# A four-block transformer in one launch: background pieces are no longer issued between the score passes of the second block's attention

## The chip, the cores and the metric

The kernel runs on one core of a Trainium2 chip. The core has a matrix engine (TensorE, "PE" in the profile, with its weight loads as "PEld"), a vector engine (VectorE, DVE), an activation engine (ScalarE, ACT), a general engine (GpSimd, POOL) and a queue that issues transfers (SyncE, SP). Each engine works off its own instructions in the order in which the program was written; semaphores order them among each other. The metric is the time of one execution on the device in microseconds (us), as the median of several runs.

## The reference, cut to what matters

Four blocks are computed one after the other on 2048 tokens of 128 numbers. Each is attention of some kind and a feed-forward part, each with a layer norm in front and its input added:

```python
    x = L0_attn_x
    x = x + _L0_attn_ref(_layernorm(x, axis=-1), ...)   # 16 heads of 8
    x = x + _L0_ffn_ref(_layernorm(x, axis=-1), ...)    # gelu, 128 -> 512 -> 128
    x = x + _L1_attn_ref(_layernorm(x, axis=-1), ...)   # 16 heads of 64
    x = x + _L1_ffn_ref(_layernorm(x, axis=-1), ...)    # gated silu, 128 -> 384 -> 128
    x = x + _L2_attn_ref(_layernorm(x, axis=-1), ...)   # each token with its two neighbours
    x = x + _L2_ffn_ref(_layernorm(x, axis=-1), ...)    # router, the best of 8 experts
    x = x + _L3_attn_ref(_layernorm(x, axis=-1), ...)   # memory with a recurrence over chunks of 64
    x = x + _L3_ffn_ref(_layernorm(x, axis=-1), ...)    # router, the best 2 of 8 experts, and a shared one
    return x
```

The attentions of the first two blocks are over all 2048 tokens:

```python
        scores = q @ k.T * scale
        attn = softmax(scores)
        out = attn @ v
```

The memory of the last block is a recurrence. Its state is carried through 32 chunks of 64 tokens: in each, the gradient of a small network's loss is taken at the state, limited in its norm, and the state moves on by it. So a chunk can't begin before the one ahead of it has ended.

## The kernel before

**Stages.** The first block's attention (`l0_attn`) comes first, with its feed-forward part and the keys and values of the second block as work in the background. Then comes the second block's attention (`l1_attn`). Its queries are cut into five blocks `QB` of 384 (392 with some edge tokens), 512, 512, 384 and 256 tokens, and its 16 heads into 8 pairs. A unit is one query block with one pair of heads; there are 40 units in the order of `SEG`. A unit has 16 steps, one for each 128 keys.

**A step.** The scores are built transposed (keys on partitions, queries along the row), for both heads `e` of the pair, in four passes `ops`: the keys' high part by the queries' high part `qhh`, by their low part `qlt`, the keys' low part by `qhh`, and the subtraction of the row maximum (`onr` by `mbt`). ACT takes the exponential into `P`. POOL (in some steps DVE) adds up the rows' sums (`do_sum`, tiles `acg` and `acd`). The products with the values (`do_pv`) of two steps are made together (`pvn=2`): in a step called `last` here (every second one, and the first) the two earlier steps' products follow. `max_upto` computes the row maxima of a unit ahead: a product of queries and keys `km` and a `TENSOR_REDUCE` into `mx` on DVE.

**Banks.** The eight PSUM banks belong to one pool `mx`. Everything that multiplies takes one (`mi`, `take`) and gives it back (`rel`).

**Background.** What comes after the attention of a finished query block is cut into pieces by generators: `stage_a` and `stage_a2` (the gated feed-forward part and the next attention's inputs), `stage_b`, `stage_b2` (neighbour attention, experts), `stage_c`, `chunk`, `stage_d` (the recurrence: coefficients, 32 chunks, output), `stage_g` (the last router). A piece ends at a `yield`. What it yields tells what the next piece needs: an int is a number of banks, "T" says that the next piece holds a product but takes no bank, "same" that it follows on DVE, a fraction that it must wait so long. The last feed-forward part (`s_lane`, `stage_e0`) runs only in the tail, when attention has ended.

**The order.** All instructions are written by one Python program, in one order; the program keeps an estimated clock `clk` for each engine. `fill(lim, only)` issues background pieces: it goes through `helpers` (pieces that belong to units: query products, maxima, the ends of units) and `parts` (the generators above, in the order of `order`), takes the first whose `may` says that it is ready by the clocks, and goes on until the clock of PE has advanced by `lim` or nothing is ready. With `only="t"`, pieces that need a bank or hold a product (`banks`, `pe`) are passed over, so that PE's order is not changed. `need` issues what must be done by now, ready or not. At a unit's end (`u_end`) the rows' sums go through DRAM to be inverted and spread (`smd`, `rcd`, `rb`), and after every second unit `stage_wo` multiplies by the output weights; its last part adds to the residual `xs` and lets the background have the block.

**Where pieces are issued in `l1_attn`.** After each of the first three passes (`ti`) with "t"; after the exponentials, in a `last` step with a full `fill()` behind the maxima and then with "t", in the others with "t" alone; after each `do_pv` with "t"; and behind the products with a full `fill()` and "t" again.

The functions as the profile numbers them:

Of the kernel before, what the change touches and what calls it, by code (L numbers as in the profile page):

```python
# [28 lines left out]
CH = 64  # L29
NCH = S // CH  # L30
ATANH = (1.0000000039388743, 0.3333315796754013, 0.20012426861749952, 0.13980709417165652, 0.14087328632693624)
T = dict(ti=(0, 1, 2), tf=1, lead0=22, more0=4, mgap=0.4, pvq=2, lim0=0.5, fq=(3,), pl=-0.5, pr=1.0, tlow=2, tback=3, late=0.3, pvp="mx", mxp="mx", ex=(256, 768, 1280, 1792, 2047), low=1, lows='ge', keep=1, leave=5, pvn=2, sp=0, rdy=40., eu=2, qg=(22, 16, 10), em=2, el=6, sem=0.2, same=1.2, tsame=3.0, order="hdmBbAaEcCeg", ps=dict(mx=8), dma=2.3, slack=0.1, lim=0.6, backlog=2.5, lead=(10, 8, 6), pp=9, dve=(6, 7, 14, 15), qp=(1, 1), lanes=2, xl=5,
         QB=[(0, 384, 392), (384, 512, 512), (896, 512, 512), (1408, 384, 384), (1792, 256, 256)])


# [35 lines left out]
def body(ctx: ExitStack, tc: tile.TileContext, x, pa, pb, pc, pi, pd, pr, pr0, pe, pw, out):  # L71
# [16 lines left out]
    leave = [0]  # L88
    mode = [None]
    L1COST = {"T": (0.0, 1 / 2400), "A": (0.12, 1 / 1200), "D": (0.1, 1 / 960), "P": (0.15, 1 / 530)}  # L90
    COST = {"T": (0.0, 1 / 2400), "A": (0.09, 1 / 1200), "D": (0.04, 1 / 960), "P": (0.15, 1 / 460)}

# [3 lines left out]
    def note(eng, op, a, k):  # L96
# [7 lines left out]
        if eng == "S":  # L104
            clk["S"] = max(clk["S"], clk["T"]) + 0.55
            end = max(t, clk["S"]) + T["dma"]
        else:
            big = max(ins + outs, key=lambda v: math.prod(v.shape[1:])) if eng != "T" else outs[0]
            cols = math.prod(big.shape[1:])
            if eng == "T":  # L110
                cols *= 2 if op == "transpose" else 4 if ins[-1].dtype == F32 else 1
# [25 lines left out]
    class Eng:  # L137
# [3 lines left out]
        def __getattr__(self, name):  # L141
            f = getattr(self.e, name)

            def g(*a, **k):
# [7 lines left out]
    te, ve, se, ge, sy = (Eng(e, n) for e, n in ((nc.tensor, "T"), (nc.vector, "D"), (nc.scalar, "A"),  # L152
                                                 (nc.gpsimd, "P"), (nc.sync, "S")))
# [8 lines left out]
    pp = ctx.enter_context(tc.tile_pool(name="pp", bufs=T["pp"]))  # L162
# [15 lines left out]
    def mi():  # L178
        return take(bgpools)

    mxp = ["mx"]
# [12 lines left out]
    class Part:  # L194
# [24 lines left out]
        def step(self):  # L219
            piece[0] = clk["T"]  # L220
            r = next(self.gen, "end")
            self.same = r == "same"
            self.ready = 0.0 if self.same else piece[0] + (r if type(r) is float else 0.0)
            self.pe = r == "T" or type(r) is float
            self.banks = r if type(r) is int else 0
            self.seen = len(emitted) if r is False else -1
            if r == "end":
                emitted.add(self.key)
            return r != "end"
# [16 lines left out]
    def fill(lim=None, only=""):  # L246

        t0 = clk["T"]
        while clk["T"] - t0 < (lim or T["lim"]):
            kept[0] = 0  # L250
            h = next((h for h in helpers if h.may(only)), None)
            if h:
                if not h.step():
                    helpers.remove(h)
                continue
            st = next((s for s in parts if s.may(only)), None)
            if st is None:
                return
            if not st.step():
                parts.remove(st)  # L260
# [20 lines left out]
    def mm(o, lhsT, rhs, start=True, stop=True, **kw):  # L281
        return te.matmul(o, lhsT, rhs, start=start, stop=stop, **kw)
# [37 lines left out]
    def C(n, i=0, w=None):  # L320
        o, ww = PC[n]
        return pcs[:, o + i:o + i + (w or ww)]
# [705 lines left out]
    def stage_wo(qb, part):  # L1028

        t0, tn, n = QB[qb]  # L1030
        yield 1
        ps = mi()
        for p in range(2 * part, 2 * part + 2):
            mm(ps[:, :n], C("wo", p * 128, 128), O.pop(p)[:, :n], start=(p % 2 == 0), stop=(p % 2 == 1))
            yield "T" if p % 2 == 0 else 0
        if part == 0:
            w = l1w.tile([128, 512], F32, name="wac", tag="wac", bufs=2)
            se.activation(w[:, :n], ps[:, :n], AF.Identity, bias=bo1)
            rel(ps)
            wacc[qb] = w  # L1040
            return
        w = wacc[qb]
        ve.tensor_tensor(w[:, :n], w[:, :n], ps[:, :n], ALU.add)
        rel(ps)
        if part < NP1 // 2 - 1:
            return
        del wacc[qb]
        if n != tn:
            ne = len(EXTRA)
            xm = edge_x[0] = sm.tile([ne, 128], F32, name="xm", tag="xm", bufs=1)  # L1050
            for i, t in enumerate(EXTRA):
                sy.dma_start(xm[i:i + 1, :], xs[t % 128:t % 128 + 1, t // 128, :])
            piece[0] = clk["D"]
        yield 1
        c0, nt = t0 // 128, tn // 128
        t = mi()
        for i in range(nt):
            te.transpose(tok(t, i), tok(w, i), ident)
        yield
        ve.tensor_tensor(xs[:, c0:c0 + nt, :], xs[:, c0:c0 + nt, :],  # L1060
                         t[:, :tn].rearrange("p (c d) -> p c d", d=128), ALU.add)
        rel(t)
        emitted.add(("x", qb))
        if n != tn:
            yield 1
            t = mi()
            te.transpose(t[:ne, :128], w[:, tn:tn + ne], ident)
            yield
            ve.tensor_tensor(xm, xm, t[:ne, :128], ALU.add)
            rel(t)  # L1070
            emitted.add("xm")

    def l1_attn():
# [69 lines left out]
        for g in range(16 * U):  # L1143
            u, k = divmod(g, 16)
            qb, p = units[u]
            n = QB[qb][2]
            if k == 0:
                need(("m", u))
                need(("ql", u))
            if u + 2 < U:  # L1150
                if k == 1 and seg[u + 2] > seg[u + 1]:
                    need(("q", u + 1))
                    u_loadx(seg[u + 2])
                if k == T["qp"][n <= 256] and u + 2 >= EU:
                    helper(("q", u + 2), u_qprep(u + 2))
            if k == 2 and 1 < u + 1 < U:
                need(("q", u + 1))
                helper(("ql", u + 1), u_qlow(u + 1))
            if k % SPC == 0:
                ka, v = nxt.pop(0)  # L1160
                g2 = g + 2 * SPC
                if g2 < 16 * U:
                    nxt.append(u_loadk(g2 // 16, (g2 % 16) // SPC))
            last = len(prev) == T["pvn"] or g == 0
            if not last:

                max_upto(max_at(g + 16 + LEAD[n] + 1))
            pts = []
            ks = slice((k % SPC) * 128, (k % SPC) * 128 + 128)
            pss = [take(["mx"]) for _ in range(2)]  # L1170
            ops = ((ka[:, 0, ks], qhh[u]), (ka[:, 0, ks], qlt[u % 2]), (ka[:, 1, ks], qhh[u]), (onr, mbt[u % 2]))
            for i, (a, b) in enumerate(ops):
                for e in range(2):
                    rows = slice(64 * e, 64 * e + 64)
                    mm(pss[e][:, :n], a[rows], b[rows, :n], start=(i == 0), stop=(i == 3), par=e and 0.02)
                if T["tf"] and i in T["ti"]:
                    fill(9.0, "t")
            for e in range(2):
                pt = pp.tile([128, 512], F32, name="P", tag="P")
                se.activation(pt[:, :n], pss[e][:, :n], AF.Exp)  # L1180
                rel(pss[e])
                pts.append(pt)
            if last:
                max_upto(max_at(g + 16 + LEAD[n] + 1))
                fill()
            elif 0:
                fill()
            if T["tf"]:
                fill(9.0, "t")
            if prev:  # L1190
                do_sum(*prev[-1])
            if len(prev) == T["pvn"]:
                while prev:
                    do_pv(*prev.pop(0))
                    if T["tf"]:
                        fill(9.0, "t")
                fill()
                if T["tf"]:
                    fill(9.0, "t")
            do_merge()  # L1200
            prev.append((g, pts, v))
        do_sum(*prev[-1])
# [442 lines left out]
    def chunk(b, c):  # L1645
# [12 lines left out]
        ps = mi()  # L1658
# [18 lines left out]
        ps = mi()  # L1677
# [14 lines left out]
        ve.tensor_tensor(ef, pf, v2f, ALU.subtract)  # L1692
        ve.tensor_tensor(e2, pt, kvt[:, c, 1, :], ALU.subtract)
        ve.scalar_tensor_tensor(u, tht, 2.0, u, ALU.mult, ALU.add)
        yield "T"
        mm(da, ef, w2)
        se.activation(j1, e2, AF.Square, accum_out=rr[:, 1:2])
        acs = lt([64, 2, 32], "acs", 1, l3c)
# [17 lines left out]
        ps = mi()  # L1716
# [312 lines left out]
    order = dict(h=s_h, d=s_d, c=lambda: s_c(0), C=lambda: s_c(1), m=s_m, b=s_b, B=s_b2, a=s_a, A=s_a2, g=s_g, e=s_e0, E=s_e1)  # L2029
# [106 lines left out]
```

## Time and profile before

| | |
|---|---|
| median of 3 runs | 2923.37 us |
| lowest and highest run | 2907.05, 2929.48 us |
| the profiled execution's own time | 2913.47 us |
| its span, first to last instruction | 2911.8 us |
| its mean granted TensorE clock | 0.952 |
| PE busy | 2659.1 us, 91% |
| PEld busy | 1345.8 us, 46% |
| DVE busy | 2300.0 us, 79% |
| ACT busy | 1567.9 us, 54% |
| POOL busy | 1369.1 us, 47% |

A busy engine counts its instructions from start to end, without overlaps; matmuls are pipelined, so a busy PE is not PE at its peak. The granted clock is the share of full speed that the chip allowed TensorE. In the profile's lines `out<-in` are names of tiles, `x` a number of instructions, `[n <-R]` an idle time of n us that R ended. Nearly all instructions have the line L147, that of a helper that records them, so they are told apart by their tiles: `mi` is any PSUM bank, `ka` a block of keys and values, `km` keys for the maxima, `xst` the state of the recurrence, `acg` and `acd` the sums on POOL and DVE. Attention of the second block runs from about 929 us to 2597 us.

### The profile page before, as it was taken

How to read it: one execution, taken by the hardware profiler on the slowest of the kernel's cores; microseconds unless marked ns; L12 is line 12 of the kernel's file. 1: busy time of each engine (PE TensorE's matmuls, PEld its weight loads, DVE VectorE, ACT ScalarE, POOL GpSimd, SP SyncE). 2: the span in 40 equal slices, each digit the busy share in tenths (PEclk: the TensorE clock that was granted, in tenths of full speed). 3: DMA queues.
4: the chain of work that ended last, by engine and by line, in shares of the span. 5: the costliest groups of instructions: out<-in, count | busy, mean ns of one | idle time of the engine just before them, and what ended most of it. 6: DMA issues, size and time to landing. Idle time of an engine off the chain costs nothing.

```text
span 2911.8 us, 50046 instructions
## 1 busy us (share of the span) xinstructions
PE 2659.1 (91%) x16719; PEld 1345.8 (46%) x16719; DVE 2300.0 (79%) x4860; ACT 1567.9 (54%) x3937; POOL 1369.1 (47%) x1601
## 2 busy tenths in 40 slices
PE   6999999999988999998989999989989899989888
PEld 1222222222234455554445544445555466556666
DVE  7899888998642777787798788888788887888865
ACT  1788887887964455544444444434444345434444
POOL 3400110201124676766656668655566456735445
PEclk9999999999987999999999999999999999978879
DMA  6311231230225344432323323223333344523345
GB/s 146 74 28 17 57 101 22 79 85 19 75 93 165 113 132 140 138 113 89 100 88 93 86 92 113 91 77 95 93 105 103 98 121 124 146 66 88 87 117 123
DMA packets 248487, 276.10 MB, mean 95 GB/s; under 512 B 96355, under 2 KB 183938, under 8 KB 248102
## 3 DMA queue, kind: packets, MB, share of 16 engines
q1 hardware_dynamic: 247366, 272.71, 33.8%
q8 instruction: 133, 2.18, 0.3%
q14 instruction: 124, 1.02, 0.1%
q10 hardware_dynamic: 864, 0.20, 0.0%
HBM read 230.25 MB, written 42.28 MB: 94 GB/s over the span
## 4 chain that ended last, share of the span: by engine, by line
PE 57%; DVE 26%; ACT 6%; DMA 4%; issue 4%; POOL 1%; SPq 0%; ACTq 0%; POOLq 0%; DVEq 0%
PE mi L147 57%; DVE mx L147 8%; ACT P L147 3%; DVE acd L147 3%; DMA rb<-rcd 2%; DVE gt L147 1%; DMA rcd<-rc 1%; DVE sB L147 1%; DVE xn L147 1%; DVE xs L147 1%; DVE gq L147 1%; ACT kf L147 1%; DVE sG L147 1%; DVE o L147 1%; ACT kh L147 1%
## 5 line engine op out<-in xcount | busy, mean ns | idle before, releaser
L147 DVE TENSOR_REDUCE mx<-mi 128x1 f32<-128x512 f32 (+1 forms) x2080 | 1318.7, 681 | 392.8 <-PE mi L147 381.5
L147 ACT ACTIVATE P<-mi 128x512 f32<-128x512 f32 (+3 forms) x2304 | 1108.6, 554 | 680.1 <-PE mi L147 665.0
L147 POOL TENSOR_TENSOR acg<-acg,P 128x512 f32<-128x512 f32 (+3 forms) x800 | 851.6, 1092 | 273.7 <-ACT P L147 273.0
L147 PE MATMUL mi<-P,ka 128*64 128x512 f32 (+3 forms) x2560 | 532.9, 539 | 0.0
L147 PE MATMUL mi<-qh,ka 64*128 64x512 f32 (+3 forms) x2560 | 478.2, 362 | 28.6 <-DVE mx L147 18.9
L147 PE MATMUL mi<-kop,qop 48*128 48x512 bf16 x1024 | 346.8, 403 | 24.9 <-DVE mx L147 12.3
L147 PE MATMUL mi<-qop,kop 50*128 50x512 bf16 x1024 | 316.0, 389 | 27.7 <-ACT P L147 25.2
L147 PE MATMUL mi<-P,vop 128*32 128x512 f32 x2048 | 302.0, 617 | 13.9 <-ACT P L147 13.9
L147 PE MATMUL mi<-km,qh 64*128 64x512 f32 x1024 | 270.7, 461 | 43.5 <-DVE mx L147 32.1
L147 PEld LDWEIGHTS mi<-qh,ka 64*128 64x128 f32 x2560 | 263.1, 189 | 90.4 <-issue 35.1
L147 PEld LDWEIGHTS mi<-P,ka 128*64 128x64 f32 x2560 | 160.3, 140 | 247.5 <-issue 208.5
L147 PE MATMUL mi<-ql,ka 64*128 64x512 f32 (+3 forms) x1280 | 240.4, 353 | 0.0
L147 PE MATMUL mi<-mbt,onr 64*128 64x512 f32 (+3 forms) x1280 | 238.1, 351 | 0.4 <-DMA mbt<-mb 0.4
L147 POOL TENSOR_SCALAR vep<-mv 128x2 f32<-128x2 f32 (+1 forms) x24 | 5.5, 231 | 492.3 <-DVE mv L147 492.3
L147 POOL TENSOR_TENSOR acg<-P 128x512 f32<-128x512 f32 (+3 forms) x80 | 97.3, 1237 | 232.4 <-ACT P L147 155.0
L147 PEld LDWEIGHTS mi<-km,qh 64*128 64x128 f32 x1024 | 116.4, 188 | 187.8 <-DVE mx L147 87.8
L147 PEld LDWEIGHTS <-kop 50*128 50x128 bf16 x1024 | 63.4, 95 | 301.9 <-issue 278.3
L147 PEld LDWEIGHTS mi<-mbt,onr 64*128 64x128 f32 x1280 | 132.2, 188 | 10.9 <-DMA mbt<-mb 1.0
L147 PEld LDWEIGHTS mi<-ql,ka 64*128 64x128 f32 x1280 | 130.1, 189 | 13.8
L147 PEld LDWEIGHTS <-qop 48*128 48x128 bf16 x1024 | 72.9, 95 | 97.5 <-issue 83.0
L147 PEld LDWEIGHTS mi<-P,vop 128*32 128x32 f32 x2048 | 55.6, 108 | 119.3 <-issue 90.3
L147 POOL TENSOR_TENSOR kl<-kf,kh 128x512 f32<-128x512 f32 x32 | 40.9, 1278 | 110.8 <-ACT kh L147 82.4
(510 smaller groups left out, 3535.5 us busy)
## 6 DMA issues: line engine op xcount, KB each, us to landing
ka<-kvd SPq DMA_DIRECT2D x320, 384.0 KB
km<-khd SPq DMA_DIRECT2D x159, 256.0 KB
khd<-kh SPq DMA_DIRECT2D x32, 256.0 KB
kvd<-kh SPq DMA_DIRECT2D x32, 256.0 KB
kvd<-kl SPq DMA_DIRECT2D x32, 256.0 KB
kvd<-vt SPq DMA_DIRECT2D x16, 512.0 KB
w3s<-in_pw_dram SPq DMA_DIRECT2D x38, 192.0 KB
ka<-in_pw_dram SPq DMA_DIRECT2D x36, 192.0 KB
```

Of the source, the lines that this page charges most:

```text
L147: r = f(*a, **k)
```

## The change

The places between the score passes, after each `do_pv`, and the second look behind each full `fill()` are taken out. In a step that is not `last`, one `fill` with "t" stays behind the exponentials, with the limit `lim` (0.6) in place of 9.0. Two pieces that hold a product without taking a bank (the second product in `stage_wo`, and `da` in `chunk`) no longer say "T", and a fraction no longer counts as one, so that a `fill` with "t" may take them.

```diff
-T = dict(ti=(0, 1, 2), tf=1, lead0=22, ...
+T = dict(lead0=22, ...
...
-            self.pe = r == "T" or type(r) is float
+            self.pe = r == "T"
...
             mm(ps[:, :n], C("wo", p * 128, 128), O.pop(p)[:, :n], start=(p % 2 == 0), stop=(p % 2 == 1))
-            yield "T" if p % 2 == 0 else 0
+            yield
...
                     mm(pss[e][:, :n], a[rows], b[rows, :n], start=(i == 0), stop=(i == 3), par=e and 0.02)
-                if T["tf"] and i in T["ti"]:
-                    fill(9.0, "t")
...
             if last:
                 max_upto(max_at(g + 16 + LEAD[n] + 1))
                 fill()
-            elif 0:
-                fill()
-            if T["tf"]:
-                fill(9.0, "t")
+            else:
+                fill(T["lim"], "t")
             if prev:
                 do_sum(*prev[-1])
             if len(prev) == T["pvn"]:
                 while prev:
                     do_pv(*prev.pop(0))
-                    if T["tf"]:
-                        fill(9.0, "t")
                 fill()
-                if T["tf"]:
-                    fill(9.0, "t")
             do_merge()
...
         ve.scalar_tensor_tensor(u, tht, 2.0, u, ALU.mult, ALU.add)
-        yield "T"
+        yield
         mm(da, ef, w2)
```

More of the change, by code (lines that the diff above doesn't have):

```diff
@@ L31 @@
 ATANH = (1.0000000039388743, 0.3333315796754013, 0.20012426861749952, 0.13980709417165652, 0.14087328632693624)
-T = dict(ti=(0, 1, 2), tf=1, lead0=22, more0=4, mgap=0.4, pvq=2, lim0=0.5, fq=(3,), pl=-0.5, pr=1.0, tlow=2, tback=3, late=0.3, pvp="mx", mxp="mx", ex=(256, 768, 1280, 1792, 2047), low=1, lows='ge', keep=1, leave=5, pvn=2, sp=0, rdy=40., eu=2, qg=(22, 16, 10), em=2, el=6, sem=0.2, same=1.2, tsame=3.0, order="hdmBbAaEcCeg", ps=dict(mx=8), dma=2.3, slack=0.1, lim=0.6, backlog=2.5, lead=(10, 8, 6), pp=9, dve=(6, 7, 14, 15), qp=(1, 1), lanes=2, xl=5,
+T = dict(lead0=22, more0=4, mgap=0.4, pvq=2, lim0=0.5, fq=(3,), pl=-0.5, pr=1.0, tlow=2, tback=3, late=0.3, pvp="mx", mxp="mx", ex=(256, 768, 1280, 1792, 2047), low=1, lows='ge', keep=1, leave=5, pvn=2, sp=0, rdy=40., eu=2, qg=(22, 16, 10), em=2, el=6, sem=0.2, same=1.2, tsame=3.0, order="hdmBbAaEcCeg", ps=dict(mx=8), dma=2.3, slack=0.1, lim=0.6, backlog=2.5, lead=(10, 8, 6), pp=9, dve=(6, 7, 14, 15), qp=(1, 1), lanes=2, xl=5,
          QB=[(0, 384, 392), (384, 512, 512), (896, 512, 512), (1408, 384, 384), (1792, 256, 256)])
```

## The prediction

> **What bounds the kernel now.** I read the page's slices first, then the busy time of three stages, then the waits of the middle stage, then two stretches of the timeline. The first 929 us (the first layer) hold nothing that the diff touches. The three stages behind are these (columns: stretch, its length, busy us and instructions of PE, PEld, DVE, ACT, POOL, granted PE clock, DMA share, GB/s):
>
> ```profile
> 929.00:1340.00 411.00, 394.25 (x2669) 218.91 (x2666) 311.16 (x512) 198.27 (x463) 287.24 (x282) 0.99 0.41 123
> 1340.00:2597.00 1257.00, 1161.77 (x7672) 654.61 (x7671) 1045.35 (x2284) 549.06 (x1622) 768.54 (x863) 0.96 0.35 101
> 2597.00:2911.80 314.80, 268.97 (x1397) 205.81 (x1393) 219.71 (x757) 136.47 (x488) 146.11 (x228) 0.84 0.40 98
> ```
>
> The first row is attention of the second layer, nearly all of it before the first query block enters `xs` (at 1286.89): PE is idle 17 us of 411. In the second the layers behind it run as background beside attention: PE idle 95 us, DVE busy 83%. The third is the tail, what is left of the background when attention has ended: PE idle 46 us, and a clock of 0.84. So PE sets the pace, and a change of order can move only the idle time and the clock. What PE waits for in the middle stage (us in total, times, longest):
>
> ```profile
> PEld mi L147 <- DVE mx L147: 110.7, 132, 6.7
> ...
> PE mi L147 <- DVE mx L147: 52.6, 37, 6.4
> ```
>
> PE waits for DVE's row maxima `mx`, which free the product banks; in the same view POOL's sums `acg` wait 316.3 us for the exponentials `P`, a quarter of the stage. The longest of these waits, in the timeline:
>
> ```profile
> 2159.66 3.87 POOL L147 TENSOR_TENSOR acg<-acg,P 128x384 f32<-128x384 f32 x4
> 2159.74 6.41 DVE L147 SCALAR_TENSOR_TENSOR u<-tht,u 64x32 f32<-64x32 f32 x1
> ...
> 2167.74 1.21 DVE L147 TENSOR_REDUCE mx<-mi 128x1 f32<-128x512 f32 x2
> ...
> 2168.42 0.68 PE L147 MATMUL mi<-qh,ka 64*128 64x384 f32 x1 [6.42 <-DVE mx L147]
> ```
>
> A background operation `u`, which takes 0.17 us elsewhere (at 2425.14), lasts 6.41 us while POOL adds; two maxima stand behind it, and PE stands behind them. A chunk of the recurrence in the background, from the same view:
>
> ```profile
> 2418.49 0.29 PE L147 MATMUL mi<-kf,xst 32*32 32x64 f32 x2
> ...
> 2419.68 0.20 DVE L147 SCALAR_TENSOR_TENSOR af<-thf,mi 32x64 f32<-32x64 f32 x1
> ...
> 2422.93 0.29 PE L147 MATMUL mi<-af,xst 32*32 32x64 f32 x2
> ...
> 2428.02 0.30 PE L147 MATMUL mi<-w2n,ef 32*64 32x32 f32 x2
> ```
>
> `af` is done at 2419.9, its product starts 3 us later: matmul pieces are let in at two places per pair of steps only. Three chunks lie between the copies of the state at 2417.72 and 2480.23, 20.8 us each. A pair of steps there takes 4.7 us (score passes of odd steps start at 2421.56 and, two pairs later, at 2430.88: 9.3 / 2 = 4.7).
>
> **The change, part by part.**
>
> Removed: the calls of `fill` between the score passes, after each of the two `do_pv`, and behind both plain fills. A pair of steps (one `last`, one not) has 13 places for background pieces now; 3 stay, one behind the exponentials of the odd step (pieces without a bank) and the two plain ones. Nothing is computed more or less, and no DMA is added; a DMA that a piece issues moves with its piece on SP's queue, behind at most one pair's loads of `ka` and `km`.
>
> (a) First layer: `fill` with "t" stays there, and its "T" marks are not edited. 0 us. The edit of `self.pe` concerns pieces that yield a number with a fraction; only `s_lane` does, and it starts in the tail, where fills take everything. 0 us; cover is not needed.
>
> (b) 929 to 1340: only the helpers of attention's own units are filled in. They are needed a unit later. 0, between -3 and +5 (a third of the 17 us idle).
>
> (c) The places behind `do_pv`: no operation of attention on ACT, DVE or POOL is issued between them and the plain fill that follows (but for a copy of `o` at a unit's end), so a piece keeps its place in those queues. 0, unless the plain fill ends on its limit of 0.6 us with pieces left; these then go one step later, which is part of (f).
>
> (d) Pieces between the passes of the `last` step now stand behind that step's maxima instead of ahead. That lets `mx` go first. Bounds: 0, and -53 us (all of PE's waits for `mx` gone). The longest wait comes from an operation of 6 us, which would only change its neighbour; I take -5.
>
> (e) DVE's operations beside POOL. In the middle stage three groups of DVE are slow; two of them (busy us, mean ns | idle before):
>
> ```profile
> L147 DVE TENSOR_TENSOR gq<-i,dO 32x64 f32<-32x64 f32 x12 | 20.2, 1682 | 0.2
> ...
> L147 DVE TENSOR_SCALAR dz<-dzr,rr 64x32 f32<-64x32 f32 x21 | 16.4, 783 | 0.9 <-POOL rr L147 0.8
> ```
>
> Against 0.22 us for its sister with the other rows (2299.99) `gq` loses 12 x 1.46 = 17.5 us; `dz` against its median of 227 ns 11.7; `u` (21 at 690 ns) against 170 ns 10.9: 40 us. A piece moved from the passes, where POOL waits for `P`, to behind the exponentials, where POOL adds for 4 x 1.07 us a pair, meets POOL more often. Bounds: 0 and +40 (twice as often). I take about a third, since only six of the 13 places lie between passes, and not all of their pieces are DVE's: +12.
>
> The Trainium skill ("SBUF — State Buffer", section "SBUF: two separate sides") says that VectorE and GpSimd share a port pair as an exclusive lock, and that whichever operation starts second is blocked while the other one runs. It speaks against the change, but by it a meeting would cost one add, about 1 us, where the row shows 6.41 us across four adds and more; by the rule, with one meeting of 1.07 us for each of the 54 operations above, the bound would be 58 us in place of 40.
>
> (f) The background advances more slowly. An ACT piece that follows a matmul piece of the second plain fill was issued before the passes end, and now stands behind two exponentials; its DVE successor then misses the next matmul place. One miss a chunk is half a pair: 2.35 us of 20.8, 11%. Block 3 of the queries enters `xs` at 2347.79, attention ends at 2597: 249 us x 0.11 = 27 us late. The block before it entered at 1984.48 and was worked off until 2480, 496 us, and would end 55 us later, in the way of block 3. Bounds: 0 (nothing misses, as in the chunk above) and 27 + 55 = 82; I take 50. In the tail:
>
> ```profile
> 2320.00:2597.00 277.00, 16.65 (x120) 10.31 (x120) 1.66 (x8) 1.44 (x8) 0.94 0.46 123
> 2597.00:2735.00 138.00, 17.25 (x116) 10.75 (x116) 1.69 (x8) 1.43 (x8) 0.82 0.31 76
> ```
>
> These rows count the recurrence alone (tile `xst`; no POOL column): 8 copies of the state on DVE before the end of attention, 8 behind it up to 2735, and 4 more. So 20 of the 32 chunks are done ahead of it. The first copy in the tail starts at 2599.76, the eighth at 2717.33, 16.8 us each. The ninth waits for its coefficients `kcs` at 2735.11, so 17.8 us are slack. 50 us late are 50 / 20.8 = 2.4 chunks, 2.4 x 16.8 = 40 us more in the tail, less the slack: +22. Bounds: 0, and 82 / 20.8 x 16.8 - 18 = +48.
>
> (g) The second product of `stage_wo` (0.59 us, 20 times in all) and `da` of a chunk (0.30 us at 2428.02) lose their "T" and may go in at the odd step's place too. PE does them anyway: 0; it can win back at most one half pair a chunk, inside the bounds of (f).
>
> (h) Clock. The tail runs at 0.84 against 0.96. The 22 us more there are mostly waiting, in which PE work runs slower: 22 x (0.96 / 0.84 - 1) = +3, taken as +4; bounds 0 and +10.
> The skill ("TensorE: Matmul & The Clock Gate", section "HAM oscillation — how this bites in real kernels") asks for an idle gap of some 3.4 us before the clock halves. The tail's row has 0.84 with PE busy 85%, so here more work in the tail has a price without such gaps; by the rule this term would be 0.
>
> Sum: -5 + 12 + 22 + 4 = +33. The profiled execution took 2913.47 us around a span of 2911.8; 2946.5 after it. It lay 9.9 us under the median of the runs, 2923.37, and I forecast medians: **2956 us**, 1.1% slower.
>
> **Rivals.**
>
> No difference: the pace of the background is set by the two matmul places, which stay. For it: the chunk above, where `af` waits 3 us for its place; DVE at 83%, which issues nothing sooner for being told sooner. Against it: 20.8 us for a chunk with four matmul pieces is over four pairs, so some pieces do miss a place. (f) and (h) fall away, (d) and (e) are left: 2923 + 7 = 2930 us.
>
> Faster: maxima come first. If most of PE's 53 us of waits for `mx` are due to pieces between the passes, half goes: -26. With it goes clock: 0.96 over 1257 us is 50 us at a loss, of which a third is -17. It decides when the lateness of (f) stays under the slack of 17.8 us. 2923 - 43 = 2880 us. Against it: the pieces still stand in the same queue, ahead of the next maxima.
>
> Much slower: the ends of the units. Behind each of the 40 units but the last a reciprocal goes through DRAM; the chain of waits shows 2.77 us (`rcd`) and 3.38 us (`rb`) at 1009.58. If later pieces let the next unit run into both each time, that is 6.15 x 39 = 240 us, and with one unit in three +80: 3003 us. Against it: nearly a unit of room, since the code asks for the finished `o` only at the next unit's last product.
>
> **How the numbers follow.** Forecast 0.55 (own range 2935 to 3000), no difference 0.25, faster 0.15, much slower 0.05. The runs of before spread over 0.8%, so 1% is what a measurement can tell. Slower by over 1% (above 2952.6): 0.42 of the forecast and 0.05, 0.47. Within 1%: 0.13 of the forecast, 0.25, and 0.01 of the faster case, 0.39. Faster: 0.14. The range from 2895 to 3010 leaves out some 0.1 below and 0.07 above.
>
> **What would show it.** Right: the first 1340 us as before within 5 us; fewer than 20 copies of `xst` ahead of the end of attention, and over 12 behind it; a tail of 335 us or more; means of `gq`, `u` and `dz` up. Wrong: a tail of 315 us or less, or 20 copies ahead of it; then (f) is nothing. A middle stage with PE idle under 75 us would be the faster case.

## The result, and the profile after

The changed kernel takes 2968.49 us (median of 4 runs, 2964.29 to 2974.91) against 2926.43 us for the kernel before on the same chip: a ratio of 1.0156, with a 95% interval of 1.0127 to 1.0186. It is slower, by more than the 1.1% forecast; the predicted 2956 us is 12 us low. The profiled execution took 2964.29 us around a span of 2962.6 us, 50.8 us more than before. The medians lie 42 us apart: the execution of before that was profiled is 13 us under its median, that of after 4 us.

Section 1 of the page of after (busy us, share of the span, instructions of each engine):

```profile
PE 2686.7 (91%) x16719; PEld 1359.4 (46%) x16719; DVE 2293.9 (77%) x4852; ACT 1557.0 (53%) x3942; POOL 1374.5 (46%) x1609
```

PE does the same 16719 products and is busy 27.6 us longer over them (2659.1 before). The other 23.2 of the 50.8 us are time in which PE is idle. The mean granted clock is 0.945 against 0.952. The same three stages as before, each cut at its own end of attention (columns: stretch, its length, busy us and instructions of PE, PEld, DVE, ACT, POOL, granted PE clock, DMA share, GB/s):

```profile
929.00:1340.00 411.00, 403.15 (x2724) 223.96 (x2724) 307.39 (x517) 201.43 (x470) 289.15 (x283) 1.00 0.42 126
1340.00:2604.00 1264.00, 1153.66 (x7492) 647.74 (x7492) 1005.50 (x2138) 522.46 (x1544) 759.02 (x850) 0.95 0.34 98
2604.00:2962.60 358.60, 295.27 (x1508) 221.45 (x1504) 255.59 (x888) 147.83 (x561) 158.13 (x248) 0.82 0.35 87
```

The exact end of attention, its last addition of sums, is at 2593.03 in before and 2603.78 in after. For before the two later stages, cut at 2593, read:

```profile
1340.00:2593.00 1253.00, 1157.77 (x7656) 652.04 (x7657) 1042.45 (x2271) 547.58 (x1612) 767.83 (x862) 0.96 0.35 101
2593.00:2911.80 318.80, 272.97 (x1411) 208.39 (x1407) 222.61 (x771) 137.94 (x498) 146.81 (x229) 0.83 0.40 98
```

The middle stage is 11 us longer, the tail 40 us. In the middle DVE has 133 operations fewer and in the tail 117 more: background work has gone over into the tail, as far as the columns can show it. PE's idle time in the middle rises from 95 to 110 us, and a view of the waits there says where (after; waited for, us in total, times, longest):

```profile
POOL acg L147 <- ACT P L147: 366.9, 129, 15.8
...
DVE mx L147 <- PE mi L147: 189.1, 139, 6.4
PEld mi L147 <- DVE mx L147: 119.4, 124, 6.4
...
PE mi L147 <- DVE mx L147: 65.7, 44, 6.0
```

PE and its weight loads wait 185 us for the row maxima, against 163 us before (110.7 + 52.6). DVE itself waits more for PE's products: 189.1 us, against 130.0. So PE and DVE both wait more for each other.

**Where the 50.8 us come from.** The background of query block 3 (chunks 21 to 28 of the recurrence) and of the last block (chunks 29 to 32) can be followed by five operations on DVE: the addition of block 3 to the residual `xs`, the first coefficients `kcs` of block 3, the copies of the state `xst` that end chunk 21 and chunk 28, and the first coefficients of the last block. From the timelines of after:

```profile
2339.47 0.54 DVE L147 TENSOR_TENSOR xs<-xs,mi 128x384 f32<-128x384 f32 x1
...
2629.39 0.28 DVE L147 TENSOR_TENSOR kcs<-kvt,ce 64x128 f32<-64x128 f32 x1
...
2648.95 0.21 DVE L147 COPY xst<-mi 64x64 f32<-64x64 f32 x1
...
2771.76 0.28 DVE L147 TENSOR_TENSOR kcs<-kvt,ce 64x128 f32<-64x128 f32 x1
...
2786.01 0.22 DVE L147 COPY xst<-mi 64x64 f32<-64x64 f32 x1 [0.41 <-PE mi L147]
```

And from those of before, where the last two stand the other way round:

```profile
2347.79 0.55 DVE L147 TENSOR_TENSOR xs<-xs,mi 128x384 f32<-128x384 f32 x1
...
2568.93 0.71 DVE L147 TENSOR_TENSOR kcs<-kvt,ce 64x128 f32<-64x128 f32 x1
...
2599.76 0.21 DVE L147 COPY xst<-mi 64x64 f32<-64x64 f32 x1
...
2717.33 0.22 DVE L147 COPY xst<-mi 64x64 f32<-64x64 f32 x1 [2.28 <-PE mi L147]
...
2735.11 0.27 DVE L147 TENSOR_TENSOR kcs<-kvt,ce 64x128 f32<-64x128 f32 x1
```

Block 3 enters 8 us earlier in after, and its coefficients come 60 us later: they take 290 us in place of 221. Chunk 28 ends 68.7 us later. In before the recurrence then waited 17.8 us for the last block's coefficients; in after these wait 14.3 us for the recurrence. So 17.8 of the 68.7 us moved nothing at this meeting, and 50.9 are left. What follows once both are there takes 176.7 us in before (2911.8 - 2735.11) and 176.6 in after (2962.6 - 2786.01), so in these two profiles the loss is all there when chunk 29 can begin.

Two things qualify this sum. First, the recurrence is not the only one that is late: the last block's own coefficients come 36.7 us later too (the block enters `xs` 12.4 us later, at 2615.75 against 2603.34). So 36.7 of the 50.9 us would be there with a recurrence on time, and only 14.3 hang on the recurrence alone. Second, its 68.7 us have two parts: chunk 21 ends 49.2 us later (at 2648.95 against 2599.76), and the seven chunks from there to chunk 28 take 19.6 us each in place of 16.8, which is 19.5 us more.

### The profile page after: what moved, and what is told of

The parts are those of the page before. It is cut to its first block, busy times and chain, and to the rows that moved or that the text cites. A ratio compares the mean times of both kernels' runs of the same rounds, so it can differ in the third digit from the quotient of the medians.

```text
span 2962.6 us, 50095 instructions
## 1 busy us (share of the span) xinstructions
PE 2686.7 (91%) x16719; PEld 1359.4 (46%) x16719; DVE 2293.9 (77%) x4852; ACT 1557.0 (53%) x3942; POOL 1374.5 (46%) x1609
## 4 chain that ended last, share of the span: by engine, by line
PE 60%; DVE 24%; ACT 6%; issue 5%; DMA 3%; POOL 2%; SPq 0%; ACTq 0%; POOLq 0%; DVEq 0%
PE mi L147 60%; DVE mx L147 7%; ACT P L147 3%; DVE acd L147 3%; DVE sB L147 1%; DVE gt L147 1%; DVE xn L147 1%; DVE xs L147 1%; DVE gq L147 1%; ACT kf L147 1%; DVE dz L147 1%; DVE o L147 1%; DMA rb<-rcd 1%; DVE sc L147 1%; DVE sG L147 1%
## 5 line engine op out<-in xcount | busy, mean ns | idle before, releaser
L147 ACT ACTIVATE P<-mi 128x512 f32<-128x512 f32 (+3 forms) x2304 | 1121.5, 554 | 935.1 <-PE mi L147 909.2
L147 PE MATMUL mi<-P,ka 128*64 128x512 f32 (+3 forms) x2560 | 540.3, 545 | 0.0
L147 PE MATMUL mi<-qh,ka 64*128 64x512 f32 (+3 forms) x2560 | 488.1, 365 | 35.0 <-DVE mx L147 23.8
L147 PE MATMUL mi<-kop,qop 48*128 48x512 bf16 x1024 | 346.6, 403 | 25.0 <-DVE mx L147 12.4
L147 PEld LDWEIGHTS mi<-qh,ka 64*128 64x128 f32 x2560 | 269.5, 189 | 104.5 <-DVE mx L147 38.8
L147 POOL TENSOR_TENSOR acg<-P 128x512 f32<-128x512 f32 (+3 forms) x80 | 88.0, 1120 | 267.7 <-ACT P L147 181.6
```

The source lines that it names most:

```text
L147: r = f(*a, **k)
```

## The experiments

The theory under test: the background advances too slowly for the recurrence to be ready when attention ends. The rivals: the three places between the passes, or the others, are what matters by themselves; the edited "T" marks, costed at nothing, carry the loss; and, later, the full `fill()` ends on its limit with pieces left, which the second look used to take (leftovers). In the last four runs the leftovers were themselves the theory under test. Ratios are to before on the same chip, with 95% intervals. Twelve kernels ran.

### One part of the change at a time

**Only the places between the passes go** (before, edited):

```diff
-T = dict(ti=(0, 1, 2), tf=1, lead0=22, ...
+T = dict(ti=(), tf=1, lead0=22, ...
```

> The kernel before with ti=(): only the places between the score passes are gone; those behind each do_pv and the second looks behind the full fills stay. Theory P (the places between the passes carry the pace of the background): 2955 to 2975 us, nearly all of the 42 us, attention ends near 2600, the tail near 355 us. Theory S (what counts are the second looks, which take what a full fill leaves behind when its 0.6 us are used up): 2920 to 2940 us.

Measured: 2921.54 us, ratio 0.9987 (0.9965 to 1.0008). No difference. The coefficients of block 3 do come later:

```profile
2594.52 0.27 DVE L147 TENSOR_TENSOR kcs<-kvt,ce 64x128 f32<-64x128 f32 x1
```

that is 252 us after the block has entered, against 221, and the time doesn't move. So the places between the passes do speed this part of the background up, by 31 us here, and that is worth nothing in time. It is not the slack that takes the 31 us up: chunk 28 (2739.01) and the last block's coefficients (2758.26) both come some 22 us later than in before, 19 us apart as against 17.8, and what follows takes 164 us in place of 177.

**Only the other places go** (before, edited; the places between the passes and the marks stay):

```diff
-            elif 0:
-                fill()
-            if T["tf"]:
-                fill(9.0, "t")
+            else:
+                fill(T["lim"], "t")
...
                     do_pv(*prev.pop(0))
-                    if T["tf"]:
-                        fill(9.0, "t")
                 fill()
-                if T["tf"]:
-                    fill(9.0, "t")
```

> The kernel before with the places between the passes, but without those behind do_pv and without the second looks; marks as before. Theory P: 2920 to 2935 us, tail near 320 us. Theory S: 2955 to 2975 us, tail near 355 us.

Measured: 2925.9 us, ratio 0.9996 (0.9974 to 1.0019). No difference either; the coefficients take 237 us. Each of the two theories missed in one of these two runs: neither set of places carries the loss by itself, and each replaces the other.

**Only the marks** (before, edited):

```diff
-            self.pe = r == "T" or type(r) is float
+            self.pe = r == "T"
...
-            yield "T" if p % 2 == 0 else 0
+            yield
...
-        yield "T"
+        yield
         mm(da, ef, w2)
```

> The kernel before with only the marks edited as in the change (the second product of stage_wo, da of a chunk, the fraction). Prediction's step (g): no difference, 2915 to 2940 us. Rival: products between the passes hold up the scores, 10 us and more slower; or da goes in earlier and the recurrence gains half a pair a chunk, 10 to 20 us faster.

Measured: 2935.58 us, ratio 1.0033 (1.0018 to 1.0049): a small loss that the interval parts from nothing. Its trace shows something that bears on how to read the stages: attention ends at 2643 us, 50 us later than in before, while the tail of 295 us is 23 us shorter. About half of what one stage gains the other loses, so the length of one stage alone says little about the whole.

**The second looks come back** (after, edited, behind both full fills):

```diff
                 fill()
+                fill(9.0, "t")
```

> The changed kernel with the second looks put back behind both full fills (9.0, "t"), nothing between the passes and nothing behind do_pv. Theory P: 2955 to 2975 us, as the changed kernel. Theory S: 2920 to 2940 us.

Measured: 2947.77 us, ratio 1.0071 (1.0046 to 1.0096). This lies between the ranges of the two theories. About half of the loss is gone, with two of the ten places per pair that were taken away put back; the coefficients take 263 us.

### The marks, the limit and the order

**After with the marks of before** (the diff of the marks, turned round):

> The changed kernel with the marks of before put back ("T" in stage_wo and chunk, fractions count as products): only the places are fewer. The marks alone, put into the kernel before, cost 0.3%. If the two parts add up: 2955 to 2960 us. If the marks cost more where places are few, because products are let in at the odd step: 2935 to 2945 us. If the marks help there, as step (g) of the prediction would have it (half a pair a chunk won back): over 2968 us.

Measured: 2950.38 us, ratio 1.0087 (1.0054 to 1.012). So the places alone, both sets, cost 0.9% (between the ranges expected), and the marks the other 0.7%, by these figures twice what they cost in before. The coefficients take 289 us, the same as in after. What differs comes ahead of them: block 3 enters `xs` 15.7 us earlier than in after (2323.74), and its coefficients, chunk 28 and the last block's coefficients are all earlier by 16 to 17 us. Put into before, the new marks likewise let block 3 enter 10 us later (2357.92). With twice the limit it is the other way round, so this is an observation and not a rule.

**After with twice the limit of a fill** (`lim` holds for the two full fills and, in after, for the odd step's as well):

```diff
-... slack=0.1, lim=0.6, backlog=2.5, ...
+... slack=0.1, lim=1.2, backlog=2.5, ...
```

> The changed kernel with the limit of a full fill doubled (lim 1.2 us of PE's estimated clock in place of 0.6). Theory L (leftovers: a full fill ends when products have used up 0.6 us, and pieces without a product, of the parts that come late in the order, wait a step or two): 2920 to 2945 us, coefficients kcs of block 5 before 2610 us. Theory N (the number of looks at different clock times sets how many dependent pieces of one part get in per pair of steps): no change, 2955 to 2980 us.

Measured: 2928.47 us, ratio 1.001 (0.9993 to 1.0028). One number takes back the whole loss, as far as the interval can tell, with three places a pair in place of 13. From its timeline, and its two later stages (columns as above):

```profile
2321.22 0.56 DVE L147 TENSOR_TENSOR xs<-xs,mi 128x384 f32<-128x384 f32 x1 [1.35 <-PE mi L147]
...
2577.16 0.31 DVE L147 TENSOR_TENSOR kcs<-kvt,ce 64x128 f32<-64x128 f32 x1
...
2727.79 0.28 DVE L147 TENSOR_TENSOR kcs<-kvt,ce 64x128 f32<-64x128 f32 x1
...
2736.37 0.22 DVE L147 COPY xst<-mi 64x64 f32<-64x64 f32 x1 [1.80 <-PE mi L147]
```

```profile
1340.00:2575.00 1235.00, 1141.68 (x7513) 644.39 (x7509) 998.96 (x2191) 525.11 (x1563) 758.99 (x849) 0.96 0.36 101
2575.00:2919.60 344.60, 290.23 (x1446) 222.39 (x1446) 236.67 (x830) 140.28 (x518) 150.72 (x238) 0.79 0.36 91
```

Block 3 enters 18 us earlier than in after and its coefficients come 52 us earlier, after 256 us. Attention ends at 2575, the earliest of all, and the tail is 345 us: 26 us longer than that of before, and the sum is as before. A long tail by itself is thus no loss; its clock of 0.79 is even lower than in after. Here a slack is seen to be used up: chunk 28 ends at 2736.37, 19.0 us later than in before, the last block's coefficients come at 2727.79, and the later of the two is only 1.3 us behind that of before.

**The coefficients first** (`stage_c` ahead of the other parts, in after and in before):

```diff
-... order="hdmBbAaEcCeg", ...
+... order="hdcCmBbAaEeg", ...
```

> The changed kernel with the recurrence's coefficients (parts c and C) moved ahead in the order of the parts (hdcCmBbAaEeg). If late coefficients and the recurrence behind them make the tail longer, as step (f) says: kcs of block 5 before 2610 us, the recurrence in the tail off the path, 2920 to 2945 us. If the 42 us come from PE's idle time in the middle stage, 2960 to 2980 us.

> The kernel before with the same order hdcCmBbAaEeg. Its recurrence ends 18 us ahead of the last block's coefficients, so step (f) expects little: 2915 to 2935 us; if the coefficients of the last block also come sooner, up to 15 us faster, 2905 to 2915 us.

Measured: 2964.82 us, ratio 1.0145 (1.01 to 1.019) in after, and 2937.17 us, ratio 1.0021 (0.9992 to 1.005) in before. After isn't helped:

```profile
2330.41 0.54 DVE L147 TENSOR_TENSOR xs<-xs,mi 128x384 f32<-128x384 f32 x1
...
2647.32 0.28 DVE L147 TENSOR_TENSOR kcs<-kvt,ce 64x128 f32<-64x128 f32 x1
```

The coefficients came 18 us later than in after, 317 us behind their block. The order did act, further up: the fifth tile of coefficients, that of an earlier block, is there at 2171 us in place of 2220. But the experts' additions to `xs` for the fourth 256 tokens, the last of which start at 2293 in after, now start their last at 2365, and the seventh tile comes at 2411 against 2402: what is brought forward is paid for by the stages behind. That suits a lack in the rate of the whole background rather than in its order; it does not prove it.

### Is it the leftovers?

Doubling the limit and the second looks both help, which suits the leftovers. Four more runs were to settle it.

**Half the limit in after** (`lim=0.3`):

> The changed kernel with the limit of a full fill halved (lim 0.3 in place of 0.6). Theory L (a full fill ends on its limit and leaves pieces behind): much slower again, 3000 us or more, with fewer copies of the state ahead of the end of attention. Theory N (the number of looks counts, not what each takes): 2955 to 2980 us.

Measured: 2981.67 us, ratio 1.0175 (1.0119 to 1.0231), no clear loss beyond that of after, where the leftovers foretold one. The coefficients do come last of all kernels, 318 us behind the block, and chunk 28 ends 17 us behind the last coefficients:

```profile
2334.41 0.54 DVE L147 TENSOR_TENSOR xs<-xs,mi 128x384 f32<-128x384 f32 x1
...
2652.36 0.28 DVE L147 TENSOR_TENSOR kcs<-kvt,ce 64x128 f32<-64x128 f32 x1
...
2797.00 0.27 DVE L147 TENSOR_TENSOR kcs<-kvt,ce 64x128 f32<-64x128 f32 x1
...
2813.96 0.21 DVE L147 COPY xst<-mi 64x64 f32<-64x64 f32 x1
```

**Twice the limit in before** (`lim=1.2`):

> The kernel before with lim 1.2. If only pieces without a product are left behind by the limit, its other places take them already, and nothing changes: 2915 to 2935 us. If products are held back by the limit too, the background runs further ahead: 2890 to 2912 us, and the tail is shorter.

Measured: 2934.3 us, ratio 1.0014 (0.9993 to 1.0034). Where there are 13 places a pair, the larger limit gains nothing.

**Twice the limit in after, with the marks of before:**

> The changed kernel with lim 1.2 and the marks of before. With lim 1.2 alone it stood at 1.001 of before; the marks back were worth 0.7% with lim 0.6 and 0.3% in the kernel before. If they add up: 2900 to 2920 us, faster than both kernels. If the marks cost only where the background is late: 2920 to 2935 us.

Measured: 2940.85 us, ratio 1.0039 (1.0011 to 1.0066), above both ranges expected and no better than the 1.001 with the new marks. With the larger limit the old marks win nothing back; with the small one they won 0.7%.

**A look with "t" ahead of each full fill** (after, with the marks of before):

```diff
                 max_upto(max_at(g + 16 + LEAD[n] + 1))
+                fill(9.0, "t")
                 fill()
...
                     do_pv(*prev.pop(0))
+                fill(9.0, "t")
                 fill()
```

> The changed kernel with the marks of before, and ahead of each full fill a look that takes only pieces without a product (9.0, "t"): the looks are at the same moments of the clock, only products can no longer use up the 0.6 us first. Without it the kernel took 2950 us (1.0087). Theory L: 2920 to 2935 us. Theory N (looks at different moments): 2945 to 2960 us, no gain.

Measured: 2954.99 us, ratio 1.0068 (1.0047 to 1.009), against 1.0087 without the extra looks: the intervals overlap, so no gain is shown. Had the full fills merely ended on their limit with pieces left that hold no product, these would have gone in here.

### All fourteen together

Each row is one profiled execution; the ratio is that of the timed runs. "Coefficients" is the time from block 3's entry into `xs` to its first `kcs`, "chunk 28" the end of that chunk against the last block's first coefficients (minus: the recurrence waits for them), "tail" the span less the end of attention. "Chunk 29" tells how much later than in before the later of the two is there, so that chunk 29 can begin, and "span" how much longer the profiled execution is.

| kernel | coefficients, us | chunk 28, us | attention ends | tail, us | chunk 29, us | span, us | ratio |
|---|---|---|---|---|---|---|---|
| before | 221 | -18 | 2593 | 319 | 0 | 0 | 1 |
| before, twice the limit | 230 | -43 | 2622 | 307 | +31 | +18 | 1.0014 |
| before, coefficients first | 232 | -37 | 2610 | 334 | +33 | +32 | 1.0021 |
| before, marks only | 235 | -48 | 2643 | 295 | +46 | +26 | 1.0033 |
| before, only pass places stay | 237 | -41 | 2599 | 312 | +3 | 0 | 0.9996 |
| before, pass places go | 252 | -19 | 2593 | 329 | +23 | +11 | 0.9987 |
| after, twice the limit | 256 | +9 | 2575 | 345 | +1 | +8 | 1.001 |
| after, second looks | 263 | -16 | 2613 | 317 | +24 | +18 | 1.0071 |
| after, twice the limit, old marks | 270 | -14 | 2621 | 327 | +40 | +36 | 1.0039 |
| after, looks ahead, old marks | 286 | -12 | 2618 | 324 | +46 | +30 | 1.0068 |
| after, old marks | 289 | +15 | 2603 | 349 | +35 | +41 | 1.0087 |
| after | 290 | +14 | 2604 | 359 | +51 | +51 | 1.0156 |
| after, coefficients first | 317 | +18 | 2600 | 353 | +63 | +42 | 1.0145 |
| after, half the limit | 318 | +17 | 2601 | 376 | +79 | +65 | 1.0175 |

The first two columns sort the ratios roughly; neither attention's end nor the tail does. Up to 256 us for the coefficients the ratio is at most 1.0033; from 263 to 289 it is 1.004 to 1.009, and from 290 on 1.0145 and more. The four slowest are the four in which chunk 28 ends 14 us or more behind the last coefficients. It is an ordering and not a law: 289 and 290 us stand beside 1.0087 and 1.0156. What follows the later of the two takes 155 to 183 us in these traces, and in before and after it happens to be the same; with the marks only, chunk 29 can begin 46 us later, nearly as late as in after, and the kernel loses 0.3%. A row's profile is also one execution, from 16 us under its kernel's median (after, second looks) to 9 us above it (before, coefficients first), so its times and its ratio do not belong to the same execution.

What stays open is how two more looks or a larger limit bring the background forward. Looks behind a full fill helped (1.0156 to 1.0071, with the new marks), looks ahead of it were not shown to (1.0087 to 1.0068, with the old ones). That would suit a piece which becomes ready only through the fill's own pieces and is then missed until the next place, so that a chain of dependent pieces advances by fewer steps a pair. It was not measured, and since the two kernels differ in their marks too, they don't part the cases by themselves.

## Why the prediction was right or wrong

**Slower, because the background is worked off later: right; the way there is right only in part.** Step (f) foretold that block 3 would be worked off later, that the recurrence would use up a slack of 17.8 us, and that the rest would show in the tail. In the two profiles chunk 28 is 68.7 us late, which less 17.8 is 50.9, where the span grew by 50.8. But the slack was reckoned to coefficients of the last block that stay at 2735.11, and they moved by 36.7 us.

The lateness that (f) took, 50 us, is about that of chunk 21 (49.2 us). Two steps from there failed. It turned the 50 us into 40 in the tail, as if they were chunks to be caught up at 16.8 us each; the recurrence was held up by late coefficients, so all 49.2 stayed. And it left 16.8 us a chunk as they were: chunks 22 to 28 took 19.6, 19.5 us more in all. Why they did isn't shown; the clock in about that stretch is 0.74 (2604 to 2770 in after, the second row of the next view), where it was 0.82 (2597 to 2735).

That the 50 us are so near is partly luck, since they were built from one miss of 2.35 us in each chunk, 11%. The same three chunks that gave 20.8 us each in before, between the copies of chunks 17 and 20, take 21.7 in after (2533.54 to 2598.59), 0.8 us more. The lateness lies in the stages ahead of the recurrence: block 3 takes 290 us to its coefficients in place of 221, 31% more, and the block before it, which was to end 55 us later, ends 118 us later. Step (f) also took the whole loss from the places between the passes; the runs show that this set alone costs no time, and that the full loss needs both sets and the marks.

**One sign given for (f) was wrong.** I had asked for fewer than 20 copies of the state ahead of the end of attention, and called (f) nothing if there were 20. There are 20 in both kernels. These rows count the recurrence alone in after (tile `xst`; stretch, length, busy us and count of PE, PEld, DVE, ACT, then clock, DMA share, GB/s), and beneath them are the entry of the block before block 3 and the copies of chunks 17 and 20, the last one the last ahead of the end:

```profile
2320.00:2604.00 284.00, 21.11 (x146) 13.18 (x146) 2.11 (x10) 1.77 (x10) 0.93 0.42 113
2604.00:2770.00 166.00, 16.28 (x103) 10.05 (x103) 1.27 (x6) 1.07 (x6) 0.74 0.23 58
2770.00:2962.00 192.00, 11.30 (x81) 7.08 (x81) 1.27 (x6) 1.06 (x6) 0.89 0.45 113
```

```profile
1969.37 0.68 DVE L147 TENSOR_TENSOR xs<-xs,mi 128x512 f32<-128x512 f32 x1
...
2533.54 0.21 DVE L147 COPY xst<-mi 64x64 f32<-64x64 f32 x1
...
2598.59 0.22 DVE L147 COPY xst<-mi 64x64 f32<-64x64 f32 x1 [2.01 <-PE mi L147]
```

The twentieth copy is at 2480.23 in before and at 2598.59 in after, 118 us later, five ahead of the end. A count can't show that: chunk 21 waits for block 3's coefficients, so the count stands at 20 however early the twentieth is. I should have asked for the time of the first coefficients. There are 12 copies behind the end, where over 12 were asked for. Of this sign only the tail of 335 us or more held, with 359.

**(a), (b): right.** The first block enters `xs` at 1283.36, against 1286.89; PE is idle 8 us of 411 there, against 17.

**(d) had the wrong sign.** -5 us was taken for maxima that go first. PE and its weight loads wait 22 us more for `mx`. With it goes the rival that foretold a faster kernel, whose sign was to be under 75 us of idle PE in the middle: there are 110.

**(e) is nothing.** The groups of DVE beside POOL in the middle of after (busy us, mean ns | idle before):

```profile
L147 DVE TENSOR_SCALAR dz<-dzr,rr 64x32 f32<-64x32 f32 x20 | 24.4, 1219 | 1.8 <-POOL rr L147 1.6
L147 DVE TENSOR_TENSOR gq<-i,dO 32x64 f32<-32x64 f32 x10 | 19.2, 1922 | 0.1
...
L147 DVE SCALAR_TENSOR_TENSOR u<-tht,u 64x32 f32<-64x32 f32 x20 | 7.7, 385 | 0.0
```

By the same reckoning as for before they lose 10 x 1.70 + 20 x 0.99 + 20 x 0.215 = 41 us, where it was 40. `gq` and `dz` are slower, `u` faster, so the sign that all three means go up held for two. These three groups, at least, lose no more beside POOL than before. Without the 12 us of (e) the forecast would have been 2944 us: that it came as near as 12 us is in part an error that made up for another.

**(g) was 0 and is not.** The marks cost 0.33% alone, 10 us, and 0.7% on top of the missing places. PE's work is the same, as I argued, but a piece with a product that is let in at the odd step's place stands in PE's order ahead of attention's own products. Whether that is what costs was not measured. With twice the limit the marks cost nothing that shows (1.001 with the new, 1.0039 with the old), so the two edits don't simply add up. The traces place the loss ahead of block 3's entry where the limit is 0.6 (16 us in after, 10 in before); why it arises stays open.

**(h) was far too small.** +4 us, of bounds 0 to +10. PE's busy time grew by 27.6 us for the same products. An estimate of the time lost to the clock is (1 - clock) x length: by the rows, whose clocks are rounded, 63 against 50 us in the middle and 65 against 54 in the tail, +24 together; by the mean clocks of the whole spans, 0.945 and 0.952, 163 against 140. I had charged the clock for the tail's growth alone, and not for the middle at all. How much of it is a cause of its own, and how much only goes with a background that waits more, no run parts: with twice the limit in after the tail's clock is lower still, 0.79, and the time is that of before.

**The other rivals.** "No difference" had argued that the two places for products set the pace. They don't alone: both stayed, and the kernel lost 1.6%. That more room at the three places left was worth 1.5% says that their room does count once the others are gone. The ends of the units can't cost what the fourth case wanted: attention as a whole ends 11 us later, and it asked for +80.

By stages, +33 us was 7 for the middle, (d) and (e), and 26 for the tail, (f) and (h); measured were 11 and 40. The tail's 14 us are the larger error, and the term that was mis-sized is (f), with the clock of (h) on top: +22 us for the recurrence, where chunk 29 could begin 50.9 us later. I built the delay from the one set of places that the change moves most visibly, and took the other set at nothing, but for pieces left by the limit, because its pieces keep their place in the queues.

## What to carry to other kernels

A background that feeds a serial chain can have a slack, and lateness that stays inside it need not cost time: with twice the limit chunk 28 came 19 us later and the time stayed. So look for the two operations that meet at the chain's critical joint, and compare the times of both before and after, rather than counts or lengths of stages: in after both had moved. Check too what follows the joint; it is not constant. Two sets of issue places can each be worth nothing while both together matter, so take them away together, too, before calling either useless. When places are taken out, the amount that each remaining place may issue is a term of its own: here twice the limit made three places as good as 13.

## What the runs showed of the hardware that was not expected

The granted clock is one half in stretches in which the profile shows PE busy for most of the time. Two of before, from the view of windows (columns as above):

```profile
2585.00:2609.00 24.00, 22.14 (x89) 14.16 (x88) 17.14 (x65) 7.91 (x41) 7.35 (x15) 0.50 0.17 50
2654.00:2670.00 16.00, 13.29 (x55) 10.52 (x55) 14.46 (x48) 4.17 (x22) 8.50 (x14) 0.50 0.38 94
```

PE is busy 92% and 83% of them, and the longest idle time shortly ahead of the first is 2.93 us, at 2580.86. In the whole tail of before 107 of 319 us run at half the clock, with one idle gap over 3.4 us; in that of after 130 of 359, with two. The busy time of PE is modelled, so it can hold waiting that the profile doesn't show.

The Trainium skill ("TensorE: Matmul & The Clock Gate", section "HAM oscillation — how this bites in real kernels") puts the halving down to gaps of over some 3.4 us in which PE is idle. Here the measurement differs from what that section says of gaps: one such gap can't account for 107 us. Whether time in which PE is busy with small or waiting products counts as idle, no run tells.
